# A state-space layer and a memory layer in one program: the loads and the first in-projection weights of the prologue in another order

## The chip, the cores and the metric

The program runs on one NeuronCore of a Trainium2 chip. A time is the device time of one execution, in microseconds (us). The core has five instruction queues: TensorE (PE in the profile, its weight loads apart as PEld), VectorE (DVE), ScalarE (ACT), GpSimd (POOL) and SyncE (SP), which here only issues transfers. ScalarE can issue transfers too. All tensors are float32.

## The reference, cut to what matters

`x` has shape (2, 512, 64, 64): two images of 512 channels and 4096 pixels, read as a sequence of 4096 tokens. Each of two layers adds its output to `x`. Layer 0 is this (the names are the reference's):

```python
x = group_norm(x)                                  # 32 groups
xn = layer_norm(x, axis=channels) * ln_w + ln_b
xin, z = split(xn @ in_proj_w.T)                   # 1024 + 1024 columns
xs = silu(causal_conv4(xin) + conv_b)
dt, Bm, Cm = split(xs @ x_proj_w.T)                # 32 + 16 + 16 columns
delta = softplus(dt @ dt_proj_w.T + dt_proj_b)
A = -exp(A_log)                                    # 1024 x 16
h = exp(delta * A) * h + delta * xs * Bm           # step by step along the tokens
y = (h * Cm).sum(states) + xs * D_skip
out = (y * silu(z)) @ out_proj_w.T
```

Layer 1 normalizes the result by groups again, matches each token against 1024 memory rows, updates these rows by the tokens that chose them, and returns a softmax mixture of the new rows. The change does not touch layer 1.

## The kernel before

**Tiling.** Channels lie on the 128 partitions: 512 channels are 4 blocks (`CB`), the 1024 inner channels are 8 blocks (`DB`). The tokens of layer 0 are worked on in 32 chunks of 256 (16 for each image), one after the other. A chunk is 32 units: for each of the 8 blocks, 4 groups of 4 states each (`units`, line 741). One unit is one scan on VectorE over 4 x 256 elements (`scan`, line 804). Before it, ScalarE makes the decays exp(delta * A) into PSUM (`decay`, line 790, four ACTIVATEs into one of two buffers `dA`), and GpSimd the inputs (`feed`, line 765, tile `bu`). After it, VectorE (for some units GpSimd) multiplies by C (`weigh`, tile `hc`), and TensorE sums over the states by transposing into PSUM (`gather`, tile `yT`).

**Order.** In layer 0 every instruction goes through `InOrder` (line 43), which stamps it, so that each engine keeps the order in which the program was written. What goes on beside the scans is placed by a table (lines 911 to 937): each entry has a unit number and a function, and the function is called when the loop over units (line 939) reaches that number; all entries with a number of 0 or less are called at unit 0, in the order of the numbers. The numbers are in the dictionary `AT` (line 179). Keys that end in 1 (`u1`, `xi1`, `c1`, `o1`, `z1`, `zo1`, `soft1`, `norm1` ...) hold only for the first chunk; the others hold for the rest.

**The prologue** (lines 220 to 309, 870 to 901) is what comes before the first scan:

- The small vectors `lnw`, `lnb`, `cw`, `cbias` are loaded by SP, then the first half (u) of `win`, the in-projection weights, 2 MB (`win_load(0)`, line 231). The weights of x_proj and dt_proj (`wxp`, `wdt`), `A` and `dsk` are loaded by ScalarE's queue (lines 237 to 253). `dt_b` is read element by element: 1024 pieces of 4 bytes.
- `stats_load(0)` reads the first image once, in 16 tiles `xl` of 512 KB through 8 buffers (`bB` and `bC`), and VectorE takes the group-norm statistics (`stats_take`, two `bn_stats` on each tile). `stats_end` (line 215) makes mean and scale of them, with two small matmuls and two ScalarE functions (tile `grs`).
- `affine(0, nc.vector)` (line 279) folds `ln_w` and `ln_b` into the u half: 32 matmuls of one column (tile `pb`) give the bias `beta`, ScalarE copies it out, and VectorE multiplies `win` by `lnw`.
- `norms(0)` (line 324) loads the first chunk `x` and normalizes it: `gn` on ScalarE, mean, centring, squares, variance, root, Newton step, scaling.
- `stats_load(1)` then reads the second image for its statistics; `win_load(1)` loads the z half of the weights.
- The first `front` (line 415): in-projection `u_mm` (tile `pz`), convolution `u_conv` (tile `cv`), `u_out`, x-projection `x_mm` (tile `px`), `x_out` (tile `xd`). In the midst of it stands `affine(1, nc.gpsimd)` (line 886): the same folding for the z half, with the multiplication on GpSimd.
- `x_out` writes B and C to DRAM, and `spread` reads them back, broadcast to all partitions. Then comes delta of the first pair of blocks (`dl0[0]`: d_mm, d_abs, d_exp, d_series, d_log, d_min, d_sum; tile `q`), `start`, four `feed`s, and the first scan.

A DMA that SP issues also waits, in this program, for the completion of the DMA eight before it: eight semaphores are used in turn.

Of the kernel before, what the change touches and what calls it, by code (L numbers as in the profile page):

```python
# [8 lines left out]
F32 = mybir.dt.float32  # L9
# [9 lines left out]
P = 128  # L19
# [30 lines left out]
def kernel(  # L50
# [123 lines left out]
    with ExitStack() as l0:  # L174
# [10 lines left out]
            "back": ((2, 6, 8, 11), (2, 12, 14, 18)), "end": 23, "u1": (1, 2, 5, 8),  # L185
            "xi1": (4, 6, 7, 8), "c1": (6, 7, 11, 9), "o1": (7, 8, 12, 13), "x1": 14, "xo1": 18,
            "silu1": 13, "gate1": 7, "z1": (-7, -4, -2, -1),
            "soft1": ((-3, -2, 0, 0, 1, 3, 3), (2, 3, 3, 4, 5, 6, 7), (6, 7, 13, 14, 14, 15, 15)),
            "wo": (5, 1, 8, 7), "m": (2, 28, 28, 30, 31, 32), "gs": 12, "zo1": (-4, -3, -1, 3),
            "norm1": (-8, -5, -5, -4, -4, -4, -4, -4, -2),  # L190
# [34 lines left out]
        def win_load(h):  # L225
# [4 lines left out]

        win_load(0)

        XO = 64
        wxp = wp.tile([P, DB, XO + 2 * N], F32, name="wxp")
        nc.gpsimd.memset(wxp[:, :, R:XO], 0.0)
        xpv = xp_wT.rearrange("(db p) j -> p db j", p=P)
        nc.scalar.dma_start(wxp[:, :, :R], xpv[:, :, :R])
        nc.scalar.dma_start(wxp[:, :, XO:], xpv[:, :, R:])
        e32 = wp.tile([XO + 2 * N, 1], F32, name="e32")
        nc.gpsimd.memset(e32, 0.0)  # L240
        nc.gpsimd.memset(e32[R : R + 1], 1.0)
        wdt = wp.tile([R + 1, DI], F32, name="wdt")
        nc.scalar.dma_start(wdt[:R], dt_wT)
        nc.scalar.dma_start(
            wdt[R : R + 1].rearrange("o (db p) -> o db p", p=P), dt_b.rearrange("p db -> db p")
        )
        A = load([P, DB, N], a_log, "A", nc.scalar)
        nc.scalar.activation(A, A, AF.Exp)
        nc.scalar.mul(A, A, -1.0)

        BIG = 1e25
        nc.vector.tensor_scalar_min(A, A, -1e-22)
        dsk = load([P, DB], d_skip, "dsk", nc.scalar)


        NQ = L // (NG * T)

        def stats_load(b):
            for k in range(CB * NQ):
                xl = (bB, bC)[k % 2].tile([P, NG, T], F32, tag="bc", name="xl")  # L260
                nc.sync.dma_start(
                    xl.rearrange("p n t -> p (n t)"),
                    xv[b, :, k // NQ, k % NQ * NG * T : (k % NQ + 1) * NG * T],
                )
                yield k // NQ, k % NQ, xl

        def stats_take(cb, q, xl):
            flat = xl.rearrange("p n t -> p (n t)")
            for h in range(NG * T // TT):
                nc.vector.bn_stats(  # L270
                    st0[:, cb, q * NG * T // TT + h, :], flat[:, h * TT : (h + 1) * TT]
                )

        big = list(stats_load(0))

        JB = 2 * DB
        beta = wp.tile([P, JB], F32, name="beta")

        def affine(h, engine):
            pb = ps.tile([P, 2, T], F32, tag="mm", name="pb")  # L280
            for j in range(DB):
                for cb in range(CB):
                    nc.tensor.matmul(
                        pb[:, 0, j : j + 1], win[:, cb, (h * DB + j) * P : (h * DB + j + 1) * P],
                        lnb[:, cb : cb + 1], start=cb == 0, stop=cb == CB - 1,
                    )
            nc.scalar.copy(beta[:, h * DB : (h + 1) * DB], pb[:, 0, :DB])
            for cb in range(CB):
                half = win[:, cb, h * DI : (h + 1) * DI]
                engine.tensor_scalar(half, half, lnw[:, cb : cb + 1], None, ALU.mult)  # L290

        affine(0, nc.vector)

        dD = wp.tile([P, DB, P], F32, name="dD")
        for db in range(DB):
            for k in range(TAPS):
                nc.gpsimd.tensor_scalar_mul(cd[:, db, k], ident, cw[:, db, k : k + 1])
            nc.gpsimd.tensor_scalar_mul(dD[:, db], ident, dsk[:, db : db + 1])

        for args in big:  # L300
            stats_take(*args)
        stats_end(0)

        nbeta = wp.tile([P, DB, 1], F32, name="nbeta")
        nc.vector.tensor_scalar_mul(nbeta[:, :, 0], beta[:, :DB], -1.0)
        cws = wp.tile([P, DB, 1], F32, name="cws")
        nc.vector.tensor_reduce(cws, cw, AX.X, ALU.add)
        nc.vector.tensor_mul(cws[:, :, 0], cws[:, :, 0], beta[:, :DB])
        nc.vector.tensor_add(cbias, cbias, cws[:, :, 0])

        carry = wp.tile([P, DB, N], F32, name="carry")
        halo = wp.tile([P, DB, TAPS - 1], F32, name="halo")

        chunks = [(b, c) for b in range(B) for c in range(NCH)]
        last = len(chunks) - 1
        U = DB * G
        PR = DB // 2
        state = [{} for _ in chunks]
        sts = {}


# [552 lines left out]
        for fn in n0:  # L874
            fn()
# [352 lines left out]
```

## Time and profile before

| what | value |
|---|---|
| time of the runs, median (lowest to highest) | 5055.22 us (5054.97 to 5063.75), 3 runs |
| the profiled execution's own time | 5066.93 us |
| its span, first to last instruction | 5065.2 us |
| busy: PE, DVE, ACT, POOL | 4523.6, 4048.3, 3533.2, 3822.4 us |
| first scan starts | 130.17 us |
| first scan of the second chunk | 280.0 us |
| first scan of the last chunk | 3846.6 us |

The profile is of one execution, which took 11.7 us longer than the median of the runs shown, so differences are taken from the profile and set off against the median. Its rows read: start, duration, engine, source line, operation, written tile <- read tiles, shapes, count, and in brackets how long the engine was idle before and what released it. Nearly all of layer 0 is recorded under L36, the line of the helper that stamps it, so its groups are told apart by their tiles.

### The profile page before, as it was taken

What the parts mean: (1) busy time and instruction counts of PE and PEld (TensorE: products, weight loads), DVE (VectorE), ACT (ScalarE), POOL (GpSimd) and SP (SyncE); (2) the same over time, 40 slices, a digit from 0 to 9 for tenths busy, and PEclk for the clock granted to TensorE, in tenths of its full rate; (3) what the DMA queues carried; (4) which work ended last, traced back from release to release, by engine and by line L of the source; (5) the groups of instructions that cost most, each with busy time, mean ns of one, the idle gap of its engine ahead of it and who ended that gap; (6) DMA issues with size and microseconds to landing.
All of it is one profiled execution on the core that took longest, in us unless ns stands there. A gap on an engine that the chain in (4) does not pass through costs nothing. (4 is left out here: it accounts for less than half of the span.)

```text
span 5065.2 us, 64865 instructions
## 1 busy us (share of the span) xinstructions
PE 4523.6 (89%) x22704; PEld 3500.2 (69%) x22704; DVE 4048.3 (80%) x3390; ACT 3533.2 (70%) x8845; POOL 3822.4 (75%) x2825
## 2 busy tenths in 40 slices
PE   6888888988888899989898888888986899998999
PEld 5677777777777777777777777777775555553444
DVE  3699999999988999999999999999998755553010
ACT  1688888888888888878888888888886555551000
POOL 3799999999999999989999999999999322220000
PEclk9899999999999999999999999999997899998999
DMA  5022221122222212121122221221112344334453
GB/s 198 19 100 77 80 80 63 63 72 73 74 71 69 65 64 65 63 63 63 63 72 84 75 73 63 67 70 64 64 61 98 117 158 149 131 134 142 144 163 119
DMA packets 174400, 447.73 MB, mean 88 GB/s; under 512 B 23256, under 2 KB 77656, under 8 KB 169848
## 3 DMA queue, kind: packets, MB, share of 16 engines
q1 hardware_dynamic: 160384, 408.50, 24.0%
q0 software_dynamic: 10240, 34.61, 2.2%
q8 instruction: 179, 2.93, 0.2%
q14 instruction: 149, 1.22, 0.1%
q10 hardware_dynamic: 3448, 0.47, 0.1%
HBM read 351.63 MB, written 91.88 MB: 88 GB/s over the span
## 5 line engine op out<-in xcount | busy, mean ns | idle before, releaser
L36 POOL TENSOR_TENSOR bu<-B,du 128x1020 f32<-128x1020 f32 (+1 forms) x1152 | 2453.2, 2146 | 127.8 <-DVE dA L36 102.1
L36 ACT ACTIVATE dA<-delta,A 128x256 f32<-128x256 f32 x4096 | 1957.9, 478 | 150.5 <-DVE hc L36 39.8
L36 DVE TENSOR_TENSOR_SCAN dA<-dA,bu 128x1024 f32<-128x1024 f32 x864 | 1977.9, 2289 | 35.9 <-ACT dA L36 16.7
L36 PE MATMUL yT<-ident,hc 128*128 128x128 f32 x8192 | 1063.5, 278 | 193.0 <-DVE hc L36 109.8
L36 DVE TENSOR_TENSOR hc<-dA,C 128x1024 f32<-128x1024 f32 x864 | 1058.5, 1225 | 164.5 <-PE yT L36 76.0
L36 PEld LDWEIGHTS yT<-ident,hc 128*128 128x128 f32 x8192 | 950.2, 143 | 281.2 <-DVE hc L36 137.2
L36 PE MATMUL pz<-x,win 128*128 128x256 f32 x4096 | 938.5, 382 | 42.6 <-ACT bu L36 23.8
L36 PEld LDWEIGHTS pz<-x,win 128*128 128x128 f32 x4096 | 763.2, 191 | 153.4 <-POOL bu L36 27.8
L36 PE MATMUL po<-z,wo 128*128 128x256 f32 x2048 | 523.5, 414 | 1.8 <-DMA wo<-in_out_wT_dram 1.1
L36 PE MATMUL cv<-xi,cd 128*128 128x256 f32 x2048 | 473.6, 384 | 29.2 <-POOL xi L36 22.9
L36 PEld LDWEIGHTS po<-z,wo 128*128 128x128 f32 x2048 | 424.2, 210 | 83.3 <-issue 15.3
L1163 PE MATMUL po<-exT,win 128*128 128x512 f32 x1024 | 444.4, 597 | 20.3 <-DVE win L1146 14.3
L36 PEld LDWEIGHTS cv<-xi,cd 128*128 128x128 f32 x2048 | 382.1, 191 | 91.5 <-POOL xi L36 28.9
L1096 PE MATMUL pc<-win,xf 128*128 128x512 f32 x960 | 432.3, 592 | 0.0
L36 DVE TENSOR_TENSOR_SCAN h<-dA,bu 128x1024 f32<-128x1024 f32 x160 | 364.9, 2280 | 21.8 <-ACT dA L36 19.9
L1163 PEld LDWEIGHTS po<-exT,win 128*128 128x128 f32 x1024 | 196.1, 192 | 268.0 <-issue 268.0
L36 POOL TENSOR_TENSOR hc<-h,C 128x1024 f32<-128x1024 f32 x160 | 379.4, 2372 | 0.5 <-PE yT L36 0.5
L1070 POOL DMA_INDIRECT tab<-rows,ix x64 | 62.8, 982 | 418.2 <-DVE den L1111 398.6
L36 ACT COPY carry<-dA 128x4 f32<-128x4 f32 x810 | 130.1, 161 | 348.9 <-DVE hc L36 343.2
L1180 DVE TENSOR_TENSOR xt<-xt,po 128x512 f32<-128x512 f32 x64 | 44.0, 687 | 389.0 <-PE po L1163 373.2
L1096 PEld LDWEIGHTS pc<-win,xf 128*128 128x128 f32 x960 | 173.0, 190 | 172.2 <-issue 172.2
L36 PE MATMUL py<-ident,ys 128*128 128x128 f32 x512 | 85.8, 292 | 188.7 <-DVE q L36 70.0
(161 smaller groups left out, 5070.2 us busy)
## 6 DMA issues: line engine op xcount, KB each, us to landing
B<-bcd SPq DMA_DIRECT2D x128, 512.0 KB, 4.3
C<-bcd SPq DMA_DIRECT2D x128, 512.0 KB, 4.3
wo<-in_out_wT_dram SPq DMA_DIRECT2D x128, 512.0 KB, 5.0
exd<-exT SPq DMA_DIRECT2D x16, 2048.0 KB, 6.3
exT<-exd SPq DMA_DIRECT2D x16, 2048.0 KB, 9.2
xl<-in_x_dram SPq DMA_DIRECT2D x32, 512.0 KB, 6.3
x<-in_x_dram SPq DMA_DIRECT2D x32, 512.0 KB, 5.3
xo<-in_x_dram SPq DMA_DIRECT2D x64, 256.0 KB, 5.7
```

Of the source, the lines that this page charges most:

```text
L36: ins = call(*args, **kwargs)
L1070: nc.gpsimd.indirect_dma_start(tab, at, rows, None)
L1096: nc.tensor.matmul(pc[:, cols], xf[:, cb, i * P : (i + 1) * P], mn[:, cb, cols], start=cb == 0, stop=cb == CB - 1,)
L1163: nc.tensor.matmul(pos[j, cb], mrow[:, kb, cb * P : (cb + 1) * P], ld[j][0][:, kb], start=kb == 0, stop=kb == KB - 1,)
L1180: nc.vector.tensor_add(xt[:, cb], xt[:, cb], pos.pop((j, cb)))
```

## The change

The small weights `wxp`, `wdt`, `A`, `dsk` move from ScalarE's queue to SP's. SP now issues: the four small vectors, eight tiles `xl`, the u half of `win`, the other eight `xl`, the two chunks `x`, then `wxp` (2), `wdt` (2), `A`, `dsk`, and then the z half of `win`. `exp(A_log)` and its negation come after the statistics on ScalarE, the clamp of `A` after them on VectorE.

`affine` is split in `affine_mm` (the one-column matmuls, for any range of blocks) and `affine_out` (copy of `beta`, multiplication of `win`). For the u half the multiplication is done by ScalarE. For the z half, the matmuls of blocks 0 to 3 come after the variance of the first chunk, those of blocks 4 to 7 after the first `d_mm`, and `affine_out(1)`, with the multiplication on VectorE, is in the table at unit 0. It is no longer ahead of the last `x_mm`. The bias sum is made in a `psy` buffer (tag `yT`) in place of a `ps` one.

GpSimd makes all 32 `cd` before the 8 `dD`. The numbers in `AT` for the first chunk change; above all the z in-projection (`z1`, `zo1`) and the second chunk's normalization (`norm1`) move from before unit 0 to units 0 to 7, and the statistics of the second image end at unit 14 (`gs`) in place of 12.

```diff
-            "back": ((2, 6, 8, 11), (2, 12, 14, 18)), "end": 23, "u1": (1, 2, 5, 8),
-            "xi1": (4, 6, 7, 8), "c1": (6, 7, 11, 9), "o1": (7, 8, 12, 13), "x1": 14, "xo1": 18,
-            "silu1": 13, "gate1": 7, "z1": (-7, -4, -2, -1),
-            "soft1": ((-3, -2, 0, 0, 1, 3, 3), (2, 3, 3, 4, 5, 6, 7), (6, 7, 13, 14, 14, 15, 15)),
-            "wo": (5, 1, 8, 7), "m": (2, 28, 28, 30, 31, 32), "gs": 12, "zo1": (-4, -3, -1, 3),
-            "norm1": (-8, -5, -5, -4, -4, -4, -4, -4, -2),
+            "back": ((2, 6, 8, 11), (2, 12, 14, 18)), "end": 23, "u1": (3, 4, 7, 9),
+            "xi1": (5, 6, 8, 10), "c1": (7, 9, 10, 12), "o1": (8, 10, 11, 13), "x1": 15,
+            "xo1": 17, "silu1": 13, "gate1": 6, "z1": (1, 2, 3, 6),
+            "soft1": ((-5, -3, -3, 1, 2, 3, 3), (3, 3, 5, 5, 5, 7, 8), (7, 7, 9, 9, 15, 17, 19)),
+            "wo": (5, 1, 8, 7), "m": (2, 28, 28, 30, 31, 32), "gs": 14, "zo1": (2, 3, 4, 7),
+            "norm1": (0, 0, 0, 0, 0, 1, 1, 2, 2), "affine": 0,
...
-        win_load(0)
...
-        nc.scalar.dma_start(wxp[:, :, :R], xpv[:, :, :R])
-        nc.scalar.dma_start(wxp[:, :, XO:], xpv[:, :, R:])
...
-        nc.scalar.dma_start(wdt[:R], dt_wT)
-        nc.scalar.dma_start(
-            wdt[R : R + 1].rearrange("o (db p) -> o db p", p=P), dt_b.rearrange("p db -> db p")
-        )
-        A = load([P, DB, N], a_log, "A", nc.scalar)
-        nc.scalar.activation(A, A, AF.Exp)
-        nc.scalar.mul(A, A, -1.0)
...
-        nc.vector.tensor_scalar_min(A, A, -1e-22)
-        dsk = load([P, DB], d_skip, "dsk", nc.scalar)
...
-        affine(0, nc.vector)
...
+        big = []
+        for n, xl in enumerate(stats_load(0)):
+            big.append(xl)
+            if n == CB * NQ // 2 - 1:
+                win_load(0)
+        n0, n1 = ([fn for _, fn in norms(i)] for i in range(2))
+        n0.pop(0)()
+        n1.pop(0)()
...
+        nc.sync.dma_start(wxp[:, :, :R], xpv[:, :, :R])
+        nc.sync.dma_start(wxp[:, :, XO:], xpv[:, :, R:])
...
+        nc.sync.dma_start(wdt[:R], dt_wT)
+        nc.sync.dma_start(
+            wdt[R : R + 1].rearrange("o (db p) -> o db p", p=P), dt_b.rearrange("p db -> db p")
+        )
+        A = load([P, DB, N], a_log, "A")
+        dsk = load([P, DB], d_skip, "dsk")
+        win_load(1)
...
+        def affine_mm(h, js=range(DB)):
+            if js[0] == 0:
+                pbs[h] = psy.tile([P, HT, 2, P], F32, tag="yT", name="pb")
+                pbs[h] = pbs[h].rearrange("p a b q -> p (a b q)")
+            pb = pbs[h]
+            for j in js:
+                for cb in range(CB):
+                    nc.tensor.matmul(
+                        pb[:, j : j + 1], win[:, cb, (h * DB + j) * P : (h * DB + j + 1) * P],
+                        lnb[:, cb : cb + 1], start=cb == 0, stop=cb == CB - 1,
+                    )
+
+        def affine_out(h):
+            nc.scalar.copy(beta[:, h * DB : (h + 1) * DB], pbs.pop(h)[:, :DB])
+            for cb in range(CB):
+                half = win[:, cb, h * DI : (h + 1) * DI]
+                if h == 0:
+                    nc.scalar.mul(half, half, lnw[:, cb : cb + 1])
+                else:
+                    nc.vector.tensor_scalar(half, half, lnw[:, cb : cb + 1], None, ALU.mult)
+
+        affine_mm(0)
+        affine_out(0)
...
         for args in big:
             stats_take(*args)
         stats_end(0)
+        nc.scalar.activation(A, A, AF.Exp)
+        nc.scalar.mul(A, A, -1.0)
...
+        nc.vector.tensor_scalar_min(A, A, -1e-22)
...
-        n0, n1 = ([fn for _, fn in norms(i)] for i in range(2))
-        n0.pop(0)()
-        n1.pop(0)()
-        win_load(1)
-        for fn in n0:
+        for fn in n0[:-3]:
+            fn()
+        affine_mm(1, range(DB // 2))
+        for fn in n0[-3:]:
             fn()
...
-            lambda: affine(1, nc.gpsimd), lambda: x_mm(range(DB - 2, DB)),
+            lambda: x_mm(range(DB - 2, DB)),
...
+        dl0[0].pop(0)()
+        affine_mm(1, range(DB // 2, DB))
         for fn in dl0[0]:
             fn()
...
-        table = []
+        table = [(AT["affine"], 0, lambda: affine_out(1))]
...
-                table += [(max(at + n, 0), 3, fn) for n, fn in norms(i + 2)]
+
+                table += [
+                    (at + n if i > 0 else max(n, AT["zo1"][-1]), 3, fn) for n, fn in norms(i + 2)
+                ]
```

## The prediction

> **What bounds the kernel now.** The parts of the page came first: DVE is busy 80% of the span, POOL 75%, ACT 70%, PE 89% (ends modelled). Layer 0 is then cut by the start of each chunk's first scan. The view of busy time by stretch, for chunks 0, 1 and 2 (columns: the stretch, its length, busy time of PE, PEld, DVE, ACT, POOL with their counts, clock, DMA share, GB/s):
>
> ```profile
> 130.17:280.00 149.83, 125.22 (x651) 105.56 (x652) 113.77 (x82) 109.53 (x276) 122.29 (x88) 0.91 0.11 35
> 280.00:397.40 117.40, 104.42 (x606) 89.96 (x606) 112.54 (x76) 100.11 (x260) 113.31 (x83) 0.99 0.31 105
> 397.40:515.70 118.30, 106.42 (x609) 91.62 (x608) 112.32 (x75) 100.42 (x260) 113.14 (x83) 0.97 0.21 68
> ```
>
> From chunk 1 on, DVE and POOL are full (112.5 and 113.3 of 117.4). The order of instructions there and in layer 1 is the same in both programs; it differs only up to the start of chunk 1. So the change is worth what it moves the first scan of chunk 1 (280.0), and a shift there is carried to the end: no later stage waits for anything that keeps its own time. Two terms: the first scan (130.17), and the 149.8 of chunk 0, 32 above the 117.4 of chunk 1.
>
> The timeline before the first scan (start, duration):
>
> ```profile
> 5.15 32.77 SPq L36 DMA_DIRECT2D xl<-in_x_dram  x16
> 12.63 13.79 PE L36 MATMUL pb<-lnb,win 128*128 128x1 f32 x64 [12.63 <-DMA win<-in_in_wT_dram]
> ...
> 24.93 4.19 POOL L36 TENSOR_SCALAR cd<-ident,cw 128x128 f32<-128x128 f32 x4
> 25.17 2.90 DVE L36 TENSOR_SCALAR win<-win,lnw 128x1024 f32<-128x1024 f32 x4 [5.87 <-PE pb L36]
> ...
> 27.99 19.07 DVE L36 BATCH_NORM_STATS2 st<-xl 128x6 f32<-128x512 f32 x32
> ...
> 29.68 2.34 POOL L36 TENSOR_SCALAR cd<-ident,cw 128x128 f32<-128x128 f32 x4
> ...
> 50.53 0.27 ACT L36 ACTIVATE grs<-gs_pv,epsc 128x4 f32<-128x4 f32 x1 [23.91 <-PE gs_pv L36]
> ...
> 52.26 2.07 ACT L36 ACTIVATE x<-x,gsh,grs 128x256 f32<-128x256 f32 x4 [1.23 <-DVE gsh L36]
> ...
> 68.17 8.90 PE L36 MATMUL pz<-x,win 128*128 128x256 f32 x32 [4.58 <-DVE x L36]
> ```
>
> The statistics run without a gap, but start only at 28, because DVE first waits for PE's `pb` to scale `win`; by then xl had been landing since 13.8. Further on:
>
> ```profile
> 100.23 11.62 PE L36 MATMUL pb<-lnb,win 128*128 128x1 f32 x64
> 110.67 11.31 POOL L36 TENSOR_SCALAR win<-win,lnw 128x1024 f32<-128x1024 f32 x4 [18.85 <-PE pb L36]
> ...
> 113.75 0.47 ACT L36 ACTIVATE xd<-px,e 96x256 f32<-96x256 f32 x1 [0.40 <-PE px L36]
> ...
> 122.06 0.62 POOL L36 TENSOR_SCALAR q<-q 128x512 f32<-128x512 f32 x1
> ...
> 130.17 2.30 DVE L36 TENSOR_TENSOR_SCAN dA<-dA,bu 128x1024 f32<-128x1024 f32 x1 [4.29 <-POOL bu L36]
> ...
> 149.76 2.29 DVE L36 TENSOR_TENSOR_SCAN h<-dA,bu 128x1024 f32<-128x1024 f32 x1 [12.57 <-ACT dA L36]
> ```
>
> Here stand 11.6 us of one-column matmuls ahead of the last x_mm, then 11.3 us of scaling on POOL ahead of delta's series `q` (ACT had written its input by 118.7), and after two scans DVE waits 12.6 us for a decay, because ACT stands behind `z` copies and squares that wait for PE.
>
> **1. Loads and statistics, up to gn on x (52.26).** One xl issued alone lands 3.8 us later (29.29 to 33.09). In a full queue one lands each 1.28 (53.23, 54.49, ... 58.34), and the 2 MB of `win` took 5.12 (46.83 to 51.95). SP issues the first xl at 2.66, so it lands at 6.5; the next come more slowly at first (before: 1.95 apart), the eighth at 17; win(0) at 22.2; the sixteenth xl at 22.2 + 8 x 1.28 = 32.4. DVE needs 1.19 for each, less than 1.28, and so ends at 33.7 in place of 47.1. Aggregation and the first small matmul: the latter stands behind `pb` on PE, which now runs 22.2 + 13.8 = 36.0; gs_pv ends at 38.0. On ACT the root `grs` is queued behind the copy of beta and four scalings of 128x1024. No such row exists; the nearest are Silu in place on that shape (1.05) and Exp with a pointer scale (1.13): 4.3 in all, 36.2 to 40.5. Then grs, DVE's six small operations, gsh at 42.3.
>
> Ahead of gn on ACT now stands exp(A), which needs A. Its load is issued behind `dt_b` (1024 pieces of 4 bytes) on SP. Before, on ACT's queue, A's issue was held 8.19 us and A landed 15.7 after dt_b's issue. Now dt_b's issue waits for the fourteenth xl (29.9). Low side: dt_b starts when x and wxp are in (37.5) and drains at the best rate seen (549 of these packets in 2 us, so 3.7 us), A lands at 42 to 43. High side: 29.9 + 15.7 = 45.6. I take 43.3, nearer the low side, as no 4 KB packets of another queue alternate with it: gn at 44, -8.3 (range -10 to -6). `dsk`, win(1) (47 to 51) and the second image's xl are queued behind; win(1) is first needed at 55, dD needs dsk by 60, the second statistics have until delta's minimum at 102: hidden.
>
> **2. The first half of z's bias: 32 of the 64 passes.** It stands between variance (gn + 11.3) and the first pz; root, Newton and scaling hide 4.5 us of it. The row says 13.79 / 64 = 0.215 a pass, without quickening over 13.8 us of unbroken PE work: 6.9 us. The Trainium skill (TensorE: Matmul & The Clock Gate, What's actually happening) has the array at half clock until it has been busy for about 3.4 us. By that rule the passes would run at 0.11 after 3.4 us and the pz behind them would start warm: 5.1 + 7.2 us (32 at the later 0.226) against 6.9 + 8.9 by the rows, 3.5 us less. I take the rows, since 64 such passes did not wake the clock: +2.3.
>
> **3. The 64 passes out of x_mm's way.** px now goes through: it ends at 101.25 in place of 113.71 in the old frame, and ACT's table load (1.28 after u_out at 98.68) is done by then: -12.4.
>
> **4. From d_mm to the first scan.** Before: 116.34 to 130.17 = 13.8. Without POOL's scaling, series, minimum, sum, du and feed would take 10.4. But the work is moved to DVE at unit 0: the four scalings (2.9) wait for the second half of `pb` (4.6 to 6.9 after d_mm), and the second chunk's centring (1.21) stands behind them and before the first scan, and waits for pd and pm (3.0 to 5.7 more, by clock). That gives d_mm + 11.6 to 13.9. The Trainium skill (SBUF — State Buffer, Who interferes with whom) says that a DVE tensor_scalar in its two-port mode locks out GpSimd for the whole instruction, which speaks against putting it beside POOL's sum and du. The trace agrees: four cd took 4.19 beside DVE's scalings, else 2.34. By the row feed is 1.9 later (d_mm + 12.3), by the rule up to 2.9 (13.3); both lie under the centring. Taken: 12.8, so -1.
>
> First scan: -8.3 + 2.3 - 12.4 - 1 = **-19.4**, at 110.8. The broadcast of B lands 8.5 after the issue of bcd (114.25 to 122.74), so at 104, before feed wants it.
>
> **5. Chunk 0.** ACT's queue, followed by hand with its rows (decay 2.0, pair of z 0.82, root 1.3): after the second decay it holds e, delta, q, beta, two squares; the third decay comes at +4.4 from the first scan, the third scan at +7 (before +19.6). The root then waits some 3.5 us for the second variance, which PE does behind gather and z_mm; the z copies come one for each unit. The ninth scan comes at +34 (before +43.8). Further on, image-2 statistics and the silus fall into one stall, and unit 16 would come at +75.5 (before +91.5). So 10 are counted out and 6 less surely; PE's waits past unit 8 were not followed. Taken **-12** (range 0 to -22).
>
> **Sum.** -19.4 - 12 = -31.4: profiled execution 5066.93 to 5035.5; set off from the median, 5055.22 - 31.4 = **5023.8**.
>
> **Rivals.** (a) Chunk 0 gives nothing: the stalls of ACT come back as waits for root, e and z. For it: three chains on PE are still in one order. Against: the z_mm that blocked the third decay leave. -19.4: 5035.8. (b) Chunk 0 packs to what POOL needs, 122.3 busy plus about 2 (-26), for 5010. For it: the stall is all in its first half (unit 16 at +91.5 of 149.8, then 3.6 a unit). Against: in-order ACT work at 109.5. (c) Slower: the one SP queue. If dt_b went at the rate seen while 4 KB packets shared the engines (about 24 in 2 us, from 2 to 8 us), it would need 85 us, A would land near 123, and gn 80 late: 5103. It decides from the point where dt_b costs A 31 us more than the 43.3 assumed; before, it had finished 15.5 after issue in company. (d) The change doesn't do what it says: the first scan moves, but chunk 1 does not, since ACT's work for chunk 1 (u, x_mm, delta) in its new places ends as late as before: about 5055. Against: those places are counted in units, and the units move.
>
> **Chances.** The forecast (gain 24 to 40) 0.60, (a) with gains of 12 to 24 0.18, (b) over 40 0.12, (c) 0.04, (d) 0.06. Under 0.2% (10 us) a measurement of this kernel can't tell a difference, as runs of before lie 8.8 us apart. (a), (b) and the forecast are faster: 0.90; (d) mostly same: 0.06; (c) slower: 0.04. The range takes in the forecast, most of (a) and half of (b): 5009 to 5042.
>
> **What would show it.** Statistics from about 6.5 to 34; `grs` right behind four ACT scalings at about 40; gn at 42 to 46, released by A rather than by DVE; pz 14 to 16 us behind the variance's end; xd with no `pb` before it; POOL's `q` 2 us behind ACT's; the first scan at 108 to 113, released by DVE's own centring or POOL's bu; third scan within 8 us; chunk 0 near 138. Wrong if gn starts after 50, if the third scan waits over 10 us, or if chunk 0 keeps its 150.

## The result and the profile after

The changed kernel takes 5035.93 us (median; 5031.5 to 5043.67 in 6 runs). The kernel before, run beside it on the same chip, takes 5056.61. The ratio is 0.9961, with a 95% interval of 0.9948 to 0.9975: 0.39% faster, 20.7 us. The forecast was 5023.8, in a range of 5009 to 5042. The time lies inside the range, but on the number of rival (a): a gain of 12 to 24 us had been given a chance of 0.18, the likeliest one, 24 to 40, a chance of 0.60.

In the two profiles the span falls from 5065.2 to 5042.0, by 23.2 us. Layer 0 by chunks, in the view of busy time by stretch (chunks 0, 1 and 2 of the changed kernel):

```profile
108.94:253.90 144.96, 123.83 (x677) 107.32 (x678) 112.29 (x84) 108.03 (x274) 121.22 (x87) 0.94 0.12 40
253.90:371.30 117.40, 104.67 (x608) 90.12 (x607) 112.48 (x75) 100.09 (x260) 113.91 (x84) 0.99 0.30 105
371.30:488.70 117.40, 105.11 (x609) 91.05 (x609) 112.47 (x75) 100.59 (x260) 113.41 (x83) 0.99 0.21 68
```

The first scan is at 108.94 (130.17 before, 21.2 earlier). Chunk 0 lasts 144.96 (149.83, 4.9 shorter). So chunk 1 starts 26.1 earlier; chunk 1 itself is as long as before. Of the 26.1, 2.9 are lost in the rest of the program, which comes up again below.

The timeline of the changed kernel before its first scan:

```profile
6.98 5.09 DVE L36 BATCH_NORM_STATS2 st<-xl 128x6 f32<-128x512 f32 x8 [6.98 <-DMA xl<-in_x_dram]
...
21.46 13.78 PE L36 MATMUL pb<-lnb,win 128*128 128x1 f32 x64 [21.46 <-DMA win<-in_in_wT_dram]
22.63 10.25 DVE L36 BATCH_NORM_STATS2 st<-xl 128x6 f32<-128x512 f32 x16 [5.11 <-DMA xl<-in_x_dram]
...
35.35 4.26 ACT L36 ACTIVATE win<-win,lnw 128x1024 f32<-128x1024 f32 x4
...
39.52 0.24 ACT L36 ACTIVATE grs<-gs_pv,epsc 128x4 f32<-128x4 f32 x1
41.52 0.65 ACT L36 ACTIVATE A<-A 128x128 f32<-128x128 f32 x2 [1.51 <-DMA A<-in_a_log_dram]
42.07 2.06 ACT L36 ACTIVATE x<-x,gsh,grs 128x256 f32<-128x256 f32 x4
...
53.18 6.83 PE L36 MATMUL pb<-lnb,win 128*128 128x1 f32 x32
...
59.87 9.96 PE L36 MATMUL pz<-x,win 128*128 128x256 f32 x32
...
94.06 0.47 ACT L36 ACTIVATE xd<-px,e 96x256 f32<-96x256 f32 x1 [1.31 <-PE px L36]
...
95.64 6.42 PE L36 MATMUL pb<-lnb,win 128*128 128x1 f32 x32
98.19 0.62 POOL L36 TENSOR_SCALAR q<-q 128x512 f32<-128x512 f32 x1 [13.61 <-ACT q L36]
100.81 4.76 DVE L36 TENSOR_SCALAR win<-win,lnw 128x1024 f32<-128x1024 f32 x4
100.96 1.73 POOL L36 TENSOR_TENSOR delta<-delta,q 128x512 f32<-128x512 f32 x1 [0.80 <-DVE q L36]
...
107.80 1.22 DVE L36 TENSOR_TENSOR x<-x,pm 128x1024 f32<-128x1024 f32 x1 [2.23 <-PE pm L36]
108.94 2.29 DVE L36 TENSOR_TENSOR_SCAN dA<-dA,bu 128x1024 f32<-128x1024 f32 x1
```

The statistics begin at 6.98 in place of 27.99 and end at 32.9. `gn` on `x` starts at 42.07 (52.26 before), right behind A. No `pb` stands between the x-projection and `xd` any more (94.06; 113.75 before). The centring of the second chunk waits 2.23 us for its mean and then releases the first scan.

Chunk 0 is where the forecast and the result part. The same view, units 2 to 5:

```profile
117.11 2.29 DVE L36 TENSOR_TENSOR_SCAN h<-dA,bu 128x1024 f32<-128x1024 f32 x1 [1.16 <-ACT dA L36]
...
121.18 0.47 ACT L36 ACTIVATE rs<-pv,epsc 128x256 f32<-128x256 f32 x1 [4.16 <-PE pv L36]
...
122.59 2.01 ACT L36 ACTIVATE dA<-delta,A 128x256 f32<-128x256 f32 x4
...
125.25 0.69 ACT L36 ACTIVATE lg<-e,one 128x512 f32<-128x512 f32 x1
...
126.04 0.69 DVE L36 SCALAR_TENSOR_TENSOR q<-lg,q 128x512 f32<-128x512 f32 x1 [6.63 <-ACT lg L36]
...
126.65 2.29 DVE L36 TENSOR_TENSOR_SCAN dA<-dA,bu 128x1024 f32<-128x1024 f32 x1
...
134.75 1.23 DVE L36 TENSOR_TENSOR hc<-dA,C 128x1024 f32<-128x1024 f32 x1 [2.29 <-PE yT L36]
```

The third scan comes 8.2 after the first, near the forecast (7). The fourth comes at 17.7, after VectorE has stood for 6.63 us. Two things it needs are on ACT behind the root `rs`, which waits 4.16 for PE: its own decay, which is ready at 124.60 (15.7 after the first scan), and the logarithm `lg`, ready at 125.94. VectorE has the minimum of the second delta, which reads `lg`, in its queue ahead of that scan. So `lg` accounts for the last 2.0 us, the root with the decay behind it for the rest. The ninth scan comes at 38.2, not at 34, and the seventeenth at 86.4, not at 75.5.

### The profile page after: what moved, and what is told of

Same layout as the page of the kernel before. It is cut to its first block, busy times and chain, and to the rows that moved or that the text cites. A ratio compares the mean times of both kernels' runs of the same rounds, so it can differ in the third digit from the quotient of the medians.

```text
span 5042.0 us, 64859 instructions
## 1 busy us (share of the span) xinstructions
PE 4516.4 (90%) x22704; PEld 3499.2 (69%) x22704; DVE 4053.2 (80%) x3390; ACT 3535.5 (70%) x8849; POOL 3822.8 (76%) x2821
## 5 line engine op out<-in xcount | busy, mean ns | idle before, releaser
L36 DVE TENSOR_TENSOR_SCAN dA<-dA,bu 128x1024 f32<-128x1024 f32 x864 | 1977.9, 2289 | 38.4 <-ACT dA L36 23.2
L36 PEld LDWEIGHTS yT<-ident,hc 128*128 128x128 f32 x8192 | 950.1, 143 | 288.4 <-DVE hc L36 139.5
L36 PE MATMUL pz<-x,win 128*128 128x256 f32 x4096 | 937.4, 382 | 33.9 <-ACT bu L36 22.4
L36 PEld LDWEIGHTS po<-z,wo 128*128 128x128 f32 x2048 | 422.7, 210 | 81.3 <-issue 15.3
L1203 DVE TENSOR_TENSOR xt<-xt,po 128x512 f32<-128x512 f32 x64 | 43.9, 686 | 388.4 <-PE po L1186 373.6
```

Source lines behind the costliest of these rows:

```text
L36: ins = call(*args, **kwargs)
L1203: nc.vector.tensor_add(xt[:, cb], xt[:, cb], pos.pop((j, cb)))
```

## The experiments

The table gives one profile for each kernel: the first scan, then the fourth, ninth and seventeenth scans counted from it, the length of chunk 0, the start of chunk 1, and the rest of the span from there on. The last column is the ratio to the kernel before, from runs on the same chip, with its 95% interval; experiments 9 and 11 have one run each, so no interval.

| kernel | first scan | 4th | 9th | 17th | chunk 0 | chunk 1 at | rest | ratio |
|---|---|---|---|---|---|---|---|---|
| before | 130.2 | 22.4 | 43.9 | 91.5 | 149.8 | 280.0 | 4785 | 1 |
| changed | 108.9 | 17.7 | 38.2 | 86.4 | 145.0 | 253.9 | 4788 | 0.9961 (0.9948-0.9975) |
| 1 loads alone | 115.8 | 23.5 | 45.0 | 92.6 | 148.9 | 264.7 | 4785 | 0.9979 (0.9969-0.9988) |
| 2 old places | 106.2 | 18.3 | 39.7 | 87.4 | 144.9 | 251.1 | 4789 | 0.9939 (0.9919-0.9959) |
| 3 logarithm first | 107.7 | 12.1 | 42.5 | 94.7 | 153.0 | 260.7 | 4780 | 0.9956 (0.9940-0.9971) |
| 4 prologue | 104.2 | 19.6 | 40.1 | 88.3 | 148.3 | 252.5 | 4779 | 0.9941 (0.9922-0.9961) |
| 5 changed again | 108.5 | 18.4 | 38.8 | 87.0 | 145.7 | 254.2 | 4791 | 0.9939 (0.9925-0.9952) |
| 6 statistics moved | 107.6 | 18.4 | 38.8 | 82.2 | 140.9 | 248.6 | 4779 | 0.9935 (0.9922-0.9949) |
| 7 Newton on VectorE | 105.7 | 20.1 | 39.6 | 87.8 | 147.9 | 253.7 | 4781 | 0.9951 (0.9937-0.9964) |
| 8 old places, 4, 6, ACT | 103.3 | 19.4 | 40.9 | 82.9 | 139.5 | 242.7 | 4791 | 0.9930 (0.9917-0.9944) |
| 9 half of z | 107.1 | 12.1 | 40.6 | 91.1 | 149.4 | 256.5 | 4774 | one run |
| 10 projections apart | 106.7 | 12.0 | 41.5 | 97.9 | 156.2 | 263.0 | 4778 | 0.9962 (0.9949-0.9976) |
| 11 hc on VectorE | 108.5 | 12.3 | 33.9 | 86.1 | 144.8 | 253.3 | 4787 | one run |
| 12 sum of 4, 6, 11 | 102.8 | 12.2 | 35.5 | 82.8 | 140.5 | 243.3 | 4784 | 0.9937 (0.9922-0.9952) |

The rest of the span lies anywhere between 4774 and 4791, though the order of instructions there is the same in all of these kernels. Two stretches of the same work (chunk 10), of experiments 6 and 8, in the view of busy time by stretch:

```profile
1316.20:1439.00 122.80, 109.68 (x618) 94.96 (x617) 113.29 (x75) 102.02 (x264) 118.26 (x88) 0.96 0.23 74
```

```profile
1313.80:1439.70 125.90, 111.51 (x618) 95.57 (x617) 113.12 (x76) 102.24 (x264) 118.27 (x88) 0.95 0.23 72
```

The same 618 matmuls take 1.8 us more and the chunk 3.1 more; the mean granted clock is 0.95 against 0.96. In chunks 9 to 11 such differences add up to 13 us (366.7 against 379.7). The runs of one kernel, in experiment 5, lie up to 17.7 us apart. So a total cannot tell changes of 5 us apart, and the experiments are read from the start of chunk 1.

**1. The loads alone.** The prologue's first part, with the z bias whole and in its old place, and the old places of chunk 0.

```diff
             lambda: x_mm(range(DB - 2)), n1[0], n1[1], lambda: u_out(3, AF.Silu),
+            lambda: affine_mm(1), lambda: affine_out(1, nc.gpsimd),
             lambda: x_mm(range(DB - 2, DB)),
...
-        affine_mm(1, range(DB // 2))
...
-        affine_mm(1, range(DB // 2, DB))
...
```

> Part 1 of the change alone: the new order of loads, the statistics started at the first xl, the u half scaled by ACT, exp(A) after the group statistics; the z half's bias is again whole and ahead of the last x_mm, its scaling again on POOL, chunk 0 keeps its old places. Theory (the terms add up): gn on x at 42 as in the changed kernel, the first scan 10 earlier than before, at 120 (118.5 to 121.5), chunk 0 again 149 to 151, so about 10 off the total (-0.2%). Rival (the time between is set by something that keeps its own time, such as the weights on the one SP queue): gn at 42, but the first scan later than 123.

`gn` starts at 42.15, 10.1 earlier than before, as expected. But the first scan is 14.4 earlier (115.8). The stages show where the other 4.3 come from: the first variance matmuls took 1.13 us (2.07 before), the first two projections `pz` 8.52 (8.90), and the z bias this:

```profile
88.59 8.86 PE L36 MATMUL pb<-lnb,win 128*128 128x1 f32 x64
```

It is 8.86 us for the 64 one-column matmuls that took 11.62 in the same place before. These matmuls were not edited. TensorE's granted clock fell from 1.00 to 0.50 later in their course: at 93.8, 5.2 us after their start, where it fell 2.2 us after it before. The total is 0.21% lower (10 us). That is the expected number, but chunk 1 starts 15.3 earlier, so the agreement is in part luck.

**2. The old places.** The changed kernel with the numbers of `AT` from before.

```diff
-            "xo1": 17, "silu1": 13, "gate1": 6, "z1": (1, 2, 3, 6),
+            "silu1": 13, "gate1": 7, "z1": (-7, -4, -2, -1),
...
-            "norm1": (0, 0, 0, 0, 0, 1, 1, 2, 2), "affine": 0,
+            "norm1": (-8, -5, -5, -4, -4, -4, -4, -4, -2), "affine": -9,
...
```

> The changed kernel with the places of chunk 0's steps as they were before (the z half's scaling ahead of them). Theory (the new places are worth the 5 us by which chunk 0 became shorter, no more): first scan at 107 to 111, the third scan again about 19 after the first in place of 8.2, the ninth at about +44, chunk 0 near 150, the total 4 to 6 above the changed kernel. Rival (the places are what lets the earlier first scan count, without them the gain of the prologue is lost in chunk 0): chunk 0 at 160 or more, total near the kernel before.

Both expectations fail. The third scan waits again, 8.47 us (15.5 after the first), in the timeline of this kernel:

```profile
93.99 3.98 PE L36 MATMUL pb<-lnb,win 128*128 128x1 f32 x32
...
106.19 2.30 DVE L36 TENSOR_TENSOR_SCAN dA<-dA,bu 128x1024 f32<-128x1024 f32 x1 [1.14 <-POOL bu L36]
...
121.67 2.29 DVE L36 TENSOR_TENSOR_SCAN h<-dA,bu 128x1024 f32<-128x1024 f32 x1 [8.47 <-ACT dA L36]
```

Yet chunk 0 is 144.9, as with the new places. So the new places gave chunk 0 nothing on balance. Chunk 1 starts 2.8 earlier than in the changed kernel (251.1), but that is not a cost of the new places: it is the earlier first scan, and 1.65 of it is there already at `xd` (92.41 against 94.06), ahead of all that was edited. Experiment 7 has the new places and its first scan at 105.7.

Under the same numbers the third scan comes at 15.5 here and at 20.7 in experiment 1. The two differ in the bias and its scaling, but also in TensorE's clock. The first 8 us of chunk 0 in experiment 1, here and in the changed kernel (the clock is the third number from the end):

```profile
115.80:123.80 8.00, 4.21 (x9) 2.48 (x9) 6.95 (x4) 3.49 (x8) 6.90 (x3) 0.62 0.10 40
```

```profile
106.19:114.19 8.00, 7.22 (x32) 5.50 (x32) 6.95 (x4) 4.68 (x12) 7.01 (x4) 1.00 0.44 177
```

```profile
108.94:116.94 8.00, 4.82 (x18) 4.44 (x19) 6.95 (x5) 5.64 (x14) 8.00 (x4) 0.51 0.29 115
```

The two variance groups and the two projections ahead of that decay took 2.08, 2.07 and 9.98 us in experiment 1 and 1.03, 1.13 and 7.17 here, 4.8 less in all, so up to 4.8 of the 5.2 can be the clock's. The comparison with the changed kernel has the same flaw. All ten profiles with the new places have a mean clock of 0.50 to 0.63 in these 8 us; experiments 2 and 8, with the old places, have 1.00. PE stands idle for 4.35 us just there in the changed kernel; whether the new places bring the low clock with them in this way was not tried.

**3. The logarithm first.** To take the 6.63 away: `lg` ahead of the root, the root behind the fourth decay, z_mm and the first u_mm one unit later.

```diff
-            "back": ((2, 6, 8, 11), (2, 12, 14, 18)), "end": 23, "u1": (3, 4, 7, 9),
+            "back": ((2, 6, 8, 11), (2, 12, 14, 18)), "end": 23, "u1": (4, 5, 7, 9),
...
-            "xo1": 17, "silu1": 13, "gate1": 6, "z1": (1, 2, 3, 6),
-            "soft1": ((-5, -3, -3, 1, 2, 3, 3), (3, 3, 5, 5, 5, 7, 8), (7, 7, 9, 9, 15, 17, 19)),
-            "wo": (5, 1, 8, 7), "m": (2, 28, 28, 30, 31, 32), "gs": 14, "zo1": (2, 3, 4, 7),
-            "norm1": (0, 0, 0, 0, 0, 1, 1, 2, 2), "affine": 0,
+            "xo1": 17, "silu1": 13, "gate1": 6, "z1": (2, 3, 4, 6),
+            "soft1": ((-5, -3, -3, 1, 1, 3, 3), (3, 3, 5, 5, 5, 7, 8), (7, 7, 9, 9, 15, 17, 19)),
+            "wo": (5, 1, 8, 7), "m": (2, 28, 28, 30, 31, 32), "gs": 14, "zo1": (3, 4, 5, 7),
+            "norm1": (0, 0, 0, 0, 0, 1, 2, 2, 2), "affine": 0,
```

> The changed kernel with four of its new places altered: the second delta's logarithm one unit earlier, so ahead of the root on ACT, the root one unit later, so behind the third decay; z_mm and the first u_mm one unit later each. Theory (what chunk 0 failed to give is the stall of the fourth scan behind lg and the root, 6.6 us): the fourth scan at +11.5 to +13 (17.7 in the changed kernel), the ninth at +32 to +34 (38.2), chunk 0 at 139 to 141, total about 5 below the changed kernel. Rival (the stall comes back later: the gate, the silus and the second image's statistics at unit 14 set the end of chunk 0's first half): fourth scan as early, but the seventeenth still at +85 to +87 and chunk 0 at 144 to 146.

The fourth scan does come at 12.1. Then more than the gain is lost: ninth scan at 42.5, chunk 0 153.0. The waits that appear, in the timeline of this kernel:

```profile
119.76 2.29 DVE L36 TENSOR_TENSOR_SCAN dA<-dA,bu 128x1024 f32<-128x1024 f32 x1
...
130.07 2.34 POOL L36 TENSOR_TENSOR hc<-h,C 128x1024 f32<-128x1024 f32 x1
132.46 1.97 PE L36 MATMUL yT<-ident,hc 128*128 128x128 f32 x8 [5.12 <-POOL hc L36]
134.52 1.23 DVE L36 TENSOR_TENSOR hc<-dA,C 128x1024 f32<-128x1024 f32 x1 [2.52 <-PE yT L36]
...
144.02 1.22 DVE L36 TENSOR_TENSOR hc<-dA,C 128x1024 f32<-128x1024 f32 x1 [6.06 <-PE yT L36]
```

The scan of unit 2 ended at 119.3, but its product with C, which GpSimd makes, starts only at 130.07. PE stands before that product's transposes for 5.12 us, and behind them in its queue are two projections (8.44 us) and the transposes that VectorE's buffers of `hc` wait for. This leaves two candidates: GpSimd's queue, or PE's projections.

**4. The prologue mended.** A and dsk loaded ahead of the x_proj weights, dt_b last; ACT's scaling of the u half behind gn; the last block of the u bias behind the group statistics; the z bias in pieces of one, three and four blocks; the second chunk's centring behind the first scan.

```diff
+        A = load([P, DB, N], a_log, "A")
+        dsk = load([P, DB], d_skip, "dsk")
         XO = 64
...
-        affine_mm(0)
-        affine_out(0)
+        affine_mm(0, range(DB - 1))
...
         stats_end(0)
+        affine_mm(0, range(DB - 1, DB))
+        for fn in n0[:3]:
+            fn()
+        affine_out(0, range(CB // 2))
+        n0[3]()
+        affine_mm(1, range(1))
...
```

> The changed kernel with its prologue altered: A and dsk loaded ahead of the x_proj weights and dt_b after the z half; ACT's scaling of the u half moved behind gn, between the squares; the last eighth of the u half's bias behind the group statistics; the z half's first four blocks of bias one after the mean, three after the variance; the second chunk's centring behind the first scan. Theory (gn waited 2.4 for ACT's scaling, 0.8 for A and 1.3 for PE's bias; the centring held the first scan by about 1): gn at 37.5 to 38.5 (42.07 in the changed kernel), variance to pz 5.2 (6.48), first scan at 101.5 to 104 (108.94), chunk 0 at 145 to 147, total 5 to 7 below the changed kernel. Rival (the first scan is held by what no edit here moves, PE's chain from pz to delta with its weights): gn early, first scan not before 106.

`gn` starts at 38.64 (42.07) and the first scan at 104.2, 4.7 earlier. But chunk 0 is 148.3, so chunk 1 starts only 1.4 earlier than in the changed kernel. With the centring behind the scan, the squares and the root come later on ACT, and the fourth scan with them (19.6).

**5. The changed kernel again.** Nothing is edited; experiment 2 had its z bias faster and its first scan earlier, and the question was whether such a difference comes from one execution to the next.

> The changed kernel once more, unaltered. In the run with the old places of chunk 0 the second half of the z bias took 3.98 us (6.42 in the changed kernel) and the first scan came 2.7 earlier, though the instructions up to the bias are the same. Theory (the granted clock falls at other places from one execution to the next): here that half takes another time than 6.42, between 3.5 and 7, and the first scan moves with it, anywhere from 105.5 to 110; the offsets inside chunk 0 move by up to 2. Rival (the places decide): 6.4 and 108.9 again within 0.3.

```profile
95.78 6.22 PE L36 MATMUL pb<-lnb,win 128*128 128x1 f32 x32
...
108.54 2.29 DVE L36 TENSOR_TENSOR_SCAN dA<-dA,bu 128x1024 f32<-128x1024 f32 x1
```

It repeats: 6.22 for the bias, 108.54 for the scan (0.4 from the first profile), 145.7 for chunk 0. These are close to the rival's numbers. But two executions that agree do not exclude chance, and the rival's reason, the places, fails: experiments 6 and 7 below keep the changed kernel's places and take 4.14 and 3.93. What decides when the clock falls stays open.

**6. The second image's statistics in the prologue.**

```diff
...
-            lambda: u_xi(3), lambda: u_out(2, AF.Silu), lambda: u_conv(3),
+            lambda: u_xi(3), stats_mean, lambda: u_out(2, AF.Silu), lambda: u_conv(3), stats_var,
...
+        stats_root()
         x_out()
...
-        table.append((AT["gs"], 5, lambda: stats_end(1)))
```

> The changed kernel with one thing moved: the group statistics of the second image, which stand at unit 14 of chunk 0, are made in the prologue (the two small matmuls around the last conv, the root behind ACT's table load, DVE's part in its idle time there). Theory (DVE spends 6.3 us on them at unit 14, 182.0 to 188.3, and the next decay is ready at 186.8): first scan 0.8 later at most, the fifteenth scan at +73 to +75 (79.4), the sixteenth at +77 to +79 (82.8), chunk 0 at 140 to 142, total 3 to 5 below the changed kernel. Rival (ACT's silus and table loads hold these units anyway): the sixteenth at +81 or later, chunk 0 at 144 or more.

The fifteenth scan comes at 73.8 (79.4), the sixteenth at 78.6 (82.8), chunk 0 is 140.9. Chunk 1 starts 5.3 earlier than in the changed kernel; 4.0 of that is chunk 0, as expected, and 1.3 is a first scan that came earlier with the faster bias.

```profile
180.79 0.69 DVE L36 TENSOR_TENSOR z<-py,z 128x512 f32<-128x512 f32 x1 [2.42 <-ACT z L36]
181.40 2.29 DVE L36 TENSOR_TENSOR_SCAN dA<-dA,bu 128x1024 f32<-128x1024 f32 x1
...
186.27 2.30 DVE L36 TENSOR_TENSOR_SCAN dA<-dA,bu 128x1024 f32<-128x1024 f32 x1 [1.25 <-ACT carry L36]
```

The scan now follows the gate at once; in the changed kernel it stood behind 6.3 us of statistics (182.0 to 188.3).

**7. Newton on VectorE.** The second chunk's Newton step and scaling leave GpSimd.

```diff
-            engine = nc.vector if i == 0 else nc.gpsimd
+            engine = nc.vector if i < 2 else nc.gpsimd
```

> The changed kernel with the Newton step and the scaling of the second chunk's norm on VectorE in place of GpSimd (5.0 us less for GpSimd, 2.8 more for VectorE, in the first three units of chunk 0). Theory (GpSimd sets the first eight units: it is busy 36.3 of their 38.2 us, so no place in ACT's queue can bring the ninth scan to +34): ninth scan at +33 to +35.5, chunk 0 at 140 to 143, total 3 to 5 below the changed kernel. Rival (the waits among the in-order queues of ACT, PE and VectorE set it, GpSimd follows): ninth scan at +37.5 or later, chunk 0 at 144 or more.

The theory fails: ninth scan at 39.6, with GpSimd busy 33.0 of these 39.6 us, where it was busy 36.3 of 38.2 in the changed kernel. VectorE now waits 7.4 us for the root on ACT, so the third scan comes at 17.3. Taking work from GpSimd doesn't help while ACT's root still stands ahead of what VectorE needs.

**8. Old places, mended prologue, statistics moved, and the z half scaled by ACT.**

```diff
-                if h == 0:
-                    nc.scalar.mul(half, half, lnw[:, cb : cb + 1])
-                else:
-                    nc.vector.tensor_scalar(half, half, lnw[:, cb : cb + 1], None, ALU.mult)
+                nc.scalar.mul(half, half, lnw[:, cb : cb + 1])
...
         for fn in dl0[0]:
             fn()
+        affine_out(1)
...
```

> The old places of chunk 0, the prologue altered as in the run with A and dsk loaded first, the second image's statistics in the prologue, and ACT scaling the z half ahead of the first decay in place of VectorE. Theory (the parts add up): first scan at 100 to 102.5 (106.2 with the old places, less 5 for the prologue, less 1 because GpSimd's sum and du have VectorE no longer beside them, plus 0.8), chunk 0 at 138 to 141, total 10 to 14 below the changed kernel. Rival (chunk 0 gives back what the first scan gains, as it did in the altered prologue alone, 148.3): first scan as early, chunk 0 at 145 or more, total within 6 of the changed kernel.

First scan at 103.3, 0.8 later than expected; chunk 0 139.5; chunk 1 at 242.7, 11.2 ahead of the changed kernel. Its total was expected 10 to 14 us below the changed kernel and is 4 below that of experiment 5 on the same chip (5027.39 against 5031.48). The slow chunks 9 to 11 shown above belong to the profiled execution, which took 8.1 more than the median; why the medians differ by so little is not shown. With VectorE away, GpSimd's sum and du take what they took before the change:

```profile
97.56 1.27 POOL L36 TENSOR_TENSOR delta<-delta,q 128x512 f32<-128x512 f32 x1 [0.80 <-DVE q L36]
98.90 1.27 POOL L36 TENSOR_TENSOR du<-delta,u 128x512 f32<-128x512 f32 x1
```

**9. Half of z.** Experiment 3, with each z_mm of chunk 0 over two of its four channel blocks; the other half of that sum is left out.

```diff
-        def in_proj(i, j0):
+        def in_proj(i, j0, cbs=CB):
...
-                for cb in range(CB):
+                for cb in range(cbs):
...
-                s["pz", DB + p] = in_proj(i, DB + 2 * p)
+                s["pz", DB + p] = in_proj(i, DB + 2 * p, CB if i else CB // 2)
```

> The run with the logarithm and the root moved, and with each z_mm of chunk 0 taken over only half of the input channels (the other half of that sum is left out, 1.8 us of PE for each of the four). Theory (what holds the first eight units is PE's queue, in which z_mm and u_mm now stand between the gathers that VectorE's hc needs; ACT's places alone can't help): the fourth scan as early as there (+12), no wait of hc for PE above 2 us in units 3 to 7, the ninth scan at +33 to +36 in place of 42.5. Rival (PE is only late because another engine is; the waits keep their length): ninth scan at +40 or later.

```profile
131.82 1.97 PE L36 MATMUL yT<-ident,hc 128*128 128x128 f32 x8 [7.89 <-POOL hc L36]
```

With 7 us less to do PE waits longer for the same product (7.89 in place of 5.12), whose transposes start at 131.8 (132.5 in experiment 3). The ninth scan is at 40.6, 1.9 earlier than in experiment 3, where the theory had 33 to 36: PE's projections are not the main cause.

**10. The projections apart.** A version that leaves nothing out: experiment 3 with z_mm at units 2, 4, 6, 9 and u_mm at 4, 6, 7, 10.

```diff
-            "back": ((2, 6, 8, 11), (2, 12, 14, 18)), "end": 23, "u1": (4, 5, 7, 9),
+            "back": ((2, 6, 8, 11), (2, 12, 14, 18)), "end": 23, "u1": (4, 6, 7, 10),
...
-            "xo1": 17, "silu1": 13, "gate1": 6, "z1": (2, 3, 4, 6),
+            "xo1": 17, "silu1": 13, "gate1": 6, "z1": (2, 4, 6, 9),
...
```

> The changed kernel with the logarithm before the root on ACT, the root after the third decay, and z_mm at units 2, 4, 6 and 9 (1, 2, 3 and 6) and u_mm at 4, 6, 7 and 10 (3, 4, 7 and 9), so that two projections never stand together ahead of a gather; nothing is left out. Theory (PE's queue holds the first eight units): fourth scan at +12 to +13, ninth at +33 to +36 (38.2), seventeenth at +81 to +86 (86.4), as the silus and the statistics of units 13 and 14 stay; chunk 0 at 141 to 145, total 1 to 4 below the changed kernel. Rival (as with the logarithm alone): ninth at +38 or later, chunk 0 at 145 or more.

Ninth scan at 41.5, chunk 0 156.2: a miss on every number but the fourth scan, and in line with experiment 9.

**11. hc of unit 2 on VectorE.** Experiment 3 again, with the one product taken from GpSimd.

```diff
-            return early(k) or k % U in AT["aside"]
+            return early(k) or (k % U in AT["aside"] and k > 2)
```

> The run with the logarithm and the root moved, and with the product hc of unit 2 in chunk 0 made by VectorE like its neighbours, not by GpSimd (2.34 us less for GpSimd, 1.22 more for VectorE). There GpSimd worked without a gap from 104.3 to 132.4 and PE waited 5.12 us for its hc, with two projections and the next gathers behind the wait. Theory (once lg is out of the way GpSimd's queue is what is late, and PE hands the lateness to VectorE's hc): no wait of PE for GpSimd's hc, the ninth scan at +36.5 to +39 (42.5), chunk 0 4 to 6 shorter than its 153.0. Rival (PE's own projections set it): ninth scan at +41 or later.

The ninth scan comes at 33.9, 8.6 earlier than in experiment 3, for 2.34 us less work on GpSimd; 36.5 to 39 was expected. Step 5 of the prediction had counted 34. But it buys nothing at the end of chunk 0 (144.8). Its timeline around the tenth scan:

```profile
142.44 2.29 DVE L36 TENSOR_TENSOR_SCAN h<-dA,bu 128x1024 f32<-128x1024 f32 x1
144.03 0.38 SPq L36 DMA_DIRECT2D x<-in_x_dram  x1
...
147.78 2.07 ACT L36 ACTIVATE x<-x,gsh,grs 128x256 f32<-128x256 f32 x4 [0.66 <-DMA x<-in_x_dram]
...
149.89 2.00 ACT L36 ACTIVATE dA<-delta,A 128x256 f32<-128x256 f32 x4
151.98 2.30 DVE L36 TENSOR_TENSOR_SCAN dA<-dA,bu 128x1024 f32<-128x1024 f32 x1 [7.26 <-ACT dA L36]
```

The decay of unit 9 stands on ACT behind the third chunk's gn. That gn waits for a load into the buffer that the last z_mm of chunk 0 has just read. In the changed kernel the same gn starts at 148.32 and the tenth scan at 152.53, so a ninth scan 4.7 us sooner (142.44 against 147.10) ends in the same place. With the old places (experiment 2) that gn was at 130.41, 24.2 after the first scan in place of 39.4. That a later gn would keep the gain was not tried.

**12. The sum.** Experiments 4, 6 and 11 together.

> The run with the logarithm, the root and the hc of unit 2 moved, with the altered prologue and the second image's statistics in the prologue. Theory (each of the three keeps what it gave alone: the first scan 4 to 5 earlier, the sixteenth scan 5 earlier, chunk 0 otherwise as in the changed kernel): first scan at 102 to 105.5, chunk 0 at 139 to 142, chunk 1 starts at 242 to 246 (253.9 in the changed kernel), total 8 to 11 below the changed kernel, so a ratio to before of 0.992 to 0.994. Rival (what sets the tenth scan keeps its own time from the first delta on, so a first scan that comes sooner only waits longer): chunk 0 at 144 or more, chunk 1 after 247.

First scan at 102.8, chunk 0 140.5, chunk 1 at 243.3: 10.6 ahead of the changed kernel. That is more than the 7.3 that the three gave one by one (1.4, 5.3 and 0.6): here chunk 0 doesn't give the earlier first scan back, as it did in experiment 4. In the total it is 0.63% faster than the kernel before, but the interval overlaps with those of the changed kernel (0.9961 and 0.9939). Experiments 8 and 12 are the best versions by the start of chunk 1. By their total they beat the kernel before, and they are not separated from the changed kernel.

## Why the prediction was right and where it was wrong

**The start of the first scan.** Steps 1 to 4 summed to -19.4; measured -21.2. Of the difference, 0.9 is in none of the steps: the first d_mm took 1.13 in place of 2.07, as the clock was still at 1.00.

- Step 1: gn at 44 forecast, 42.07 measured. The statistics ran as forecast (6.98 to 32.9; 6.5 to 33.7), and so did ACT's scaling (4.26; 4.3). The difference is A: it landed at 41.5, not at 43.3. `dt_b` was issued at 34.4, later than the 29.9 of the high side, but A landed 7.1 after that in place of 15.7; its own issue took 1.4 us in place of 8.19. Rival (c), the blocked SP queue, lay far off.
- Step 2: +2.3 forecast. From the variance's end to the first pz it is 6.48 (4.57 before), and that pz took 9.96 (8.90): +3.0. The 32 matmuls took 6.83 against 6.9 taken from the row. The Trainium skill (TensorE: Matmul & The Clock Gate, What's actually happening), by which such an unbroken run would have woken the clock, would by the prediction's estimate have given 3.5 us less; the measurement decides for the row here. In experiment 2 the trace records the clock beside it: 0.50 from 49.5 to 63.2, through all 32 of these matmuls (52.27 to 59.09).
- Step 3: from pz's start to xd 45.58 before, 34.19 after. Less the 1.06 of the slower pz this is -12.45, with -12.4 forecast.
- Step 4: d_mm's end to the first scan, 13.83 before, 13.23 after (12.8 forecast). The wait that holds it is the one named: the second chunk's mean. The Trainium skill (SBUF — State Buffer, Who interferes with whom) lets one of the two engines wait out the other's instruction. The trace agrees. The four scalings in the view by tile (ns, shortest, median and longest):

```profile
L36 DVE TENSOR_SCALAR win<-win,lnw x4: 740/1252/1759, 100.8 to 104.8; 128x1024 f32<-128x1024 f32 x4
```

The first and the last took 0.75 and 0.74 us. The two between took 1.76 and 1.75, and each ended 0.55 after GpSimd's sum or du did. The sum took 1.73 and du 1.60, in place of 1.27 each.

**Chunk 0.** Step 5 failed: -12 forecast, -4.9 measured. It was counted along ACT's queue, and there the count of the third scan was near (8.2; 7 forecast). Three things broke it, each shown by a run or a row:

- The count took `lg` as if nobody waited for it. VectorE's minimum stood ahead of the fourth scan, and `lg` behind the root and the fourth decay. That is 2.0 of the 6.63 us; the rest is the root's wait for PE, which the count had at 3.5 and which took 4.16, and the decay behind it.
- With `lg` and the decay ahead of the root (experiment 3), GpSimd's product for unit 2 was late, and PE handed the lateness to VectorE. Experiments 9 and 11 tell it from PE's own work. Only with both removed does the ninth scan come at the forecast +34.
- Even then the end of chunk 0 did not move, since the tenth scan waits for another chain, the third chunk's load and gn, which the new place of z_mm had made later. "10 are counted out" took a scan that comes sooner as time that is kept.

And experiment 2 shows that the new places as a whole were worth nothing to chunk 0: 144.9 with the old ones, 145.0 with the new. That is the step's other error: I counted what they remove (a wait of 12.57) and added no price for what they move into units 1 to 6. How much of that price is PE's low clock in the first 8 us, and whether the places cause it, is open.

**The total.** That the total fell on rival (a)'s 5035.8 is in part a coincidence. Its first term was 1.8 us too small, its second (no gain in chunk 0) 4.9 too small, the rest of the span took 2.9 more in this pair of profiles, the medians differ by 2.5 less than the profiles, and the median of the kernel before was 5056.61 in place of the 5055.22 that the forecast started from.

**By parts.** At the start of chunk 1 (280.0 before): the loads alone -15.3, of which some 4 come with the clock; the z bias and its scaling another -13.6 (experiment 1 to 2), 9.6 in the first scan and 4.0 in chunk 0, and these 4.0 can all be the clock's; experiment 2 to the changed kernel +2.8, all of it in the first scan, with a slower bias (6.42 against 3.98), and not shown to be the new places.

## What to carry to other kernels

Where several engines work through fixed queues, a stall that is taken away is worth only the distance to the next wait of the same consumer: after counting along one queue, count the same units along every other engine that the consumer reads from, up to the point where the gain is to be banked. Two waits of like length hide each other, so an edit that removes one of them can look useless or harmful; remove both before giving up either. Before two orders are compared, see that TensorE's clock was the same in both. Read small gains from a point in the trace just behind the edit, when the rest of the program varies by more than the gain.

## What was not expected of the hardware

- One-column matmuls ran at very different rates under one source. The 64 of the u half took 13.8 us wherever they stand together (0.215 us each). The 32 of the second z part took between 3.73 and 6.44 us in the twelve profiles that have them, 0.12 to 0.20 each. The same kernel gave 6.42 and 6.22 in two executions. The difference goes with how long the granted clock stays at 1.00 after they begin: in the changed kernel it fell to 0.50 at 96.3, 0.6 us after their start; in experiment 3 it fell at 99.4, just after their end, and they took 3.73.
- So 0.12 is their pace at 1.00, and 0.21 that at 0.50, which experiment 2 records for the whole of the first z part (6.82 us for 32). By that pace the u half ran at 0.50 too. The views show 1.00 there, but no trace holds a record of the clock before 42 us (the changed kernel's none before 65.6), and the views count time without a record as 1.00.
- In all fourteen traces the clock stays at one value for whole multiples of 3.41 us, save in the last stretch of each (30.72 before the fall in the changed kernel, 34.13 in experiment 3). The Trainium skill (TensorE: Matmul & The Clock Gate, What's actually happening) has the activity judged in windows that run free of the kernel's start. The multiples fit such windows, and so do other moments of the fall in other kernels; two executions that agree can neither support nor refute that they run free.
- The reads of x_proj's weights held the SP queue. Their two issues took 2.38 and 3.83 us in the changed kernel, where the load of one x takes 0.38; A behind them landed at 41.5, and `gn` waited for it by some 0.8 us (DVE's `gsh` was ready at 41.2).
- VectorE and GpSimd, working side by side on the z half's scaling and on delta, took turns: two scalings of 0.75 us became 1.76 and 1.75, and GpSimd's two operations of 1.27 became 1.73 and 1.60. With the scaling on ACT (experiment 8) GpSimd is back at 1.27 us.
